# Block 1 of a two-block transformer: the arithmetic of the finished rows' layer norm on GpSimd, the context rows' mask on VectorE

## The chip, the cores and the metric

The kernel runs on one core of a Trainium2 chip. The metric is device time in microseconds (us). A core has engines that run side by side, each taking its instructions in a fixed order: PE (TensorE, matrix products and transposes; PEld is its weight load), DVE (VectorE), ACT (ScalarE), POOL (GpSimd) and SP (SyncE), which issues the transfers (DMAs) between memory and the core. Semaphores make an instruction wait for those of another engine.

## The reference

Two blocks, one after the other, on x of shape (16, 256, 512) with a context of the same shape, 16 heads of 32. Block 0 is cross attention with a mask and an MLP of width 2048. Block 1, the one that is changed, is:

```python
mask0 = 1.0 - jnp.all(x == 0, axis=2, keepdims=True).astype(x.dtype)
z = _mha(x, x, Wq1, Wk1, Wv1, mask0, causal=True)
x1 = _layernorm(x + z, ln1_g, ln1_b)
mask1 = 1.0 - jnp.all(x1 == 0, axis=2, keepdims=True).astype(x1.dtype)
z = _mha(x1, context, Wq2, Wk2, Wv2, mask1, causal=False)
x2 = _layernorm(x1 + z, ln2_g, ln2_b)
z = jnp.maximum(x2 @ fc1_w.T + fc1_b, 0.0) * mask0
z = (z @ fc2_w.T + fc2_b) * mask0
return _layernorm(x2 + z, ln3_g, ln3_b)
```

The layer norm of a row is (x - mean) / sqrt(var + eps) * gain + offset. In `_mha` the queries, keys and values are multiplied by a 0/1 mask per row; for the second attention the keys and values come from the context, so the context's rows carry mask1.

## The kernel before

**Tiles.** Two sequences of 256 rows form a group: 512 rows, four row tiles of 128 rows by 512 columns (t = 0 to 3). There are NG = 8 groups. Block 0 runs first, its attention up to about 700 us and its MLP up to about 1390. Then block 1's attention: 16 jobs (`Mha`), first eight of self-attention, one a group, then eight of cross-attention. Then block 1's MLP.

**Two streams woven together.** A job has eight units (two sequences by four sets of four heads). The main stream (`Attention.stream`) goes head by head through all jobs: scores on PE (L414), their minimum (with the causal mask, L429, or plain, L425) on DVE, the exponential on ACT (L439), transposes on PE (L455), copies to `pt` by ACT (L461) or, for one head of four in cross jobs, by DVE (L459), and at the end of a unit the product with the values (L474). The score banks in PSUM are two, so PE can be two heads ahead of the minimum and the exponential. Beside it, `feed(n)` does the projections of a job ahead of its attention: the transposes of its input rows (L283), the projections (L264), the count of valid keys (`lengths`, L1404 to L1412, DVE). `weave` interleaves the two by costs in the program text.

**The order.** PE's instructions run in the order in which the program names them (`manual_schedule` for PE alone). The other engines' orders, SP's included, are written by the tile scheduler, which places an instruction by its own estimate of the times at which its inputs are ready. On the chip every engine then keeps that order.

**The end of a unit.** `Mha.scale` (L1450, L1451) makes the reciprocal of the row sums times the mask, `finish` (L1463 to L1472) transposes the unit's result, multiplies it into `zz` on DVE (L1465) and adds it to x on GpSimd (L1472; `zz` has two buffers). After four units, half a job, two row tiles are complete, and two calls of `norm` are put into the list `later`, of which the main stream takes one per head.

**The norm of the finished rows.** `norm(t)` calls `layer_norm`: `ln_stats` (L244, L245, L247 on DVE, then the power -0.5 on GpSimd, L248), then two instructions on DVE over 128x512, L257 ((x - mean) * gain) and L258 (x * rstd + offset). In self jobs `nonzero` (L1368, DVE) reads the finished row into a scratch tile `junk` and leaves the row's mask in m1. Then SP stores the row (L1441). The store is read back eight jobs later by the cross job of the group, or by the MLP. The x tile itself is one of three, used again three jobs later.

**The context rows.** `context_rows` fetches a 128x512 row tile `cx` (L1551; three buffers, shared with `junk`), `context` multiplies it by the row mask on GpSimd (L1558) and transposes it on PE (L283). In a cross job the fetches for the next job go out as soon as a buffer is free, right after the transposes of this job's rows.

**Weights.** At the change from self to cross, and from cross to the MLP, weights are fetched into `wst` (a tag with six buffers that `pt` shares) and split into two parts on GpSimd (L195, L198).

Of the kernel before, what the change touches and what calls it, by code (L numbers as in the profile page):

```python
# [16 lines left out]
ALU = mybir.AluOpType  # L17
# [14 lines left out]
NG = B // NB  # L32
# [10 lines left out]
def kernel(ctx: ExitStack, tc: tile.TileContext, a, out):  # L43
# [7 lines left out]
    nc = tc.nc  # L51
# [22 lines left out]
    for t, at in ((0, 0), (1, P)):  # L74
        w = (t + 1) * P
        nc.gpsimd.affine_select(
            out=tri[:, at : at + w],
# [10 lines left out]
    for i in range(NB):  # L88
        own = hmask[:, i, i * HPC : (i + 1) * HPC]
        nc.gpsimd.memset(own, 1.0)  # L90
        for base, step in ((0, 1), (D - 1, -1)):
            nc.gpsimd.affine_select(
                out=own,
# [146 lines left out]
    def ln_stats(pool, src, n=4):  # L240

        st = pool.tile([P, nc.vector.BN_STATS_DIM], F32, tag="bnst", name="st")
        mv = pool.tile([P, nc.vector.BN_AGGR_DIM], F32, tag="bnmv", name="mv", bufs=n)
        nc.vector.bn_stats(st, src)  # L244
        nc.vector.bn_aggr(mv, st)  # L245
        rstd = pool.tile([P, 2], F32, tag="bnrs", name="rstd", bufs=n)
        nc.vector.tensor_scalar(rstd[:, 0:1], mv[:, 1:2], EPS, None, ALU.add)  # L247
        nc.gpsimd.tensor_tensor(out=rstd[:, 1:2], in0=rstd[:, 0:1], in1=nhalf, op=ALU.pow)  # L248
        return mv[:, 0:1], rstd[:, 1:2]

    def normalize(pool, dst, src, n=4):
        mean, rstd = ln_stats(pool, src, n)
        nc.vector.tensor_scalar(dst, src, mean, rstd, ALU.subtract, ALU.mult)

    def layer_norm(pool, x, gain, offset):
        mean, rstd = ln_stats(pool, x)
        nc.vector.scalar_tensor_tensor(x, x, mean, gain, ALU.subtract, ALU.mult)  # L257
        nc.vector.scalar_tensor_tensor(x, x, rstd, offset, ALU.mult, ALU.add)  # L258
# [9 lines left out]
    def sbuf(ph, name, bufs, side=None):  # L268
        return ph.enter_context(
            tc.tile_pool(name=name, bufs=bufs, side=side, reuse_waits="tile")  # L270
        )
# [7 lines left out]
    def transposed(dst, src, t, tag="mm"):  # L279

        ps = bank(tag, "ps_t").rearrange("p (c n) -> p c n", n=P)
        for c in range(KC):
            nc.tensor.transpose(ps[:, c, :], src[:, ts(c, P)], ident)  # L283
        split(ps, (dst[0][:, :, ts(t, P)], dst[1][:, :, ts(t, P)]))
        return 4 * T_PASS
# [274 lines left out]
    def phase1():  # L560
# [122 lines left out]
        def normal(g, tag, t):  # L683
            x = fetched.pop((g, tag, t), None)
            if x is None:
                x = fetch(g, tag, t)
            normalize(pool, x, x)
            return x
# [184 lines left out]
    class Mlp0:  # L873
# [111 lines left out]
        def normal(self, x):  # L985
            normalize(self.small[0], x, x, self.small[1])
# [379 lines left out]
    def nonzero(junk, src, m):  # L1366

        nc.vector.tensor_scalar(  # L1368
            junk, src, 0.0, None, ALU.not_equal, ALU.max, accum_out=m
        )  # L1370
# [49 lines left out]
    def block1(mlp0):  # L1420
        tables, more = {}, {}

        class Mha(Job):
# [10 lines left out]

            def norm(self, t):
                x, table = self.x[:, t, :], tables["ln2" if self.cross else "ln1"]
                layer_norm(pool, x, table[:, 0, :], table[:, 1, :])
                if not self.cross:
                    junk = pool.tile([P, C], F32, tag="t512", name="junk", bufs=3)
                    nonzero(junk, x, m1[:, self.g, t : t + 1])  # L1440
                nc.sync.dma_start(  # L1441
                    out=xd[3 if self.cross else 2][self.g][ts(t, P), :], in_=x
                )
# [40 lines left out]
        def inputs(tag):  # L1484
            return pair(mlp0.ins, tag)
# [36 lines left out]
        pool = sbuf(ctx, "work3", 2)  # L1522
# [25 lines left out]
        def context_rows(n, t):  # L1548
            if n < len(jobs) and jobs[n].cross and (n, t) not in cxs and t < G:
                cx = cxs[n, t] = pool.tile([P, C], F32, tag="t512", name="cx", bufs=3)  # L1550
                nc.sync.dma_start(out=cx, in_=of("ctx", jobs[n].g)[:, t, :])  # L1551

        def context(n, t):
            job = jobs[n]
            if t == 0:
                job.c_t = inputs("c_t")
            cx = cxs[n, t]
            nc.gpsimd.tensor_scalar(cx, cx, job.m[:, t : t + 1], None, ALU.mult)  # L1558
            cost = transposed(job.c_t, cx, t)
            context_rows(n, t + 3)  # L1560
            return cost
# [20 lines left out]
        def feed(n):  # L1582
# [5 lines left out]
            for c in range(KC):  # L1588
                ps = yield from project_t(w["q"].w, c, job.x_t)
                q, hl = halves(pool, 0, 2)  # L1590
                q0s[c] = first_token(pool, tok0, ps)
                split(ps, hl, scale=-SC if job.cross else None)
                att.keep(job, c, 0, q)
                if job.cross:
                    for t in FRONTS[c]:
                        context_rows(n, t)
                        yield context(n, t)
# [146 lines left out]
```

## Time and profile before

| | before |
|---|---|
| median of 3 runs (lowest, highest) | 2738.64 us (2737.24, 2739.17) |
| the profiled execution | 2737.66 us, span 2735.9 us |
| granted TensorE clock, mean | 0.992 |
| DVE, norm of the finished rows L257, L258 | 0.742 us each (median) |
| GpSimd, mask of a context row L1558 | 1.572 us (median), 32 times |
| GpSimd, addition of 128x512 L1656 | 1.300 us (median) |
| GpSimd, residual addition of 128x256 L1472 | 0.735 us (median) |
| GpSimd, power L248 | 0.657 us (median) |

A row of a group of instructions names the line, engine, operation and tiles and gives the duration of one. In a timeline, a line begins with the start and the duration in us, and in brackets stands how long the engine had been idle and what released it. In a list of waits, the three numbers are the total in us, the times, and the longest. L257 and L258 are in the helper that block 1's MLP also calls (32 of their 96 rows), so they are told apart by their time. Idle time of an engine costs something only if the chain of work that sets the end runs through it.

### The profile page before, as it was taken

How to read it: one execution, taken by the hardware profiler on the slowest of the kernel's cores; microseconds unless marked ns; L12 is line 12 of the kernel's file. 1: busy time of each engine (PE TensorE's matmuls, PEld its weight loads, DVE VectorE, ACT ScalarE, POOL GpSimd, SP SyncE). 2: the span in 40 equal slices, each digit the busy share in tenths (PEclk: the TensorE clock that was granted, in tenths of full speed). 3: DMA queues.
4: the chain of work that ended last, by engine and by line, in shares of the span. 5: the costliest groups of instructions: out<-in, count | busy, mean ns of one | idle time of the engine just before them, and what ended most of it. 6: DMA issues, size and time to landing. Idle time of an engine off the chain costs nothing.

```text
span 2735.9 us, 56705 instructions
## 1 busy us (share of the span) xinstructions
PE 2655.3 (97%) x19030; PEld 2244.6 (82%) x19030; DVE 2051.8 (75%) x5963; ACT 1817.4 (66%) x5278; POOL 604.7 (22%) x676
## 2 busy tenths in 40 slices
PE   8999999999899999999989999999999999999998
PEld 6777777777799999999977887877777777777787
DVE  8776667757846569999957777777678777777887
ACT  4877777778555555444547788887777777777522
POOL 2222212114401100111211111115222222114334
PEclk9999999999999999999999999999999999999999
DMA  6666556556323344443474656667566665565221
GB/s 231 189 193 182 170 170 192 183 169 174 112 114 134 126 165 167 164 169 135 160 232 163 198 191 192 196 195 224 179 198 193 190 192 184 183 187 163 100 93 51
DMA packets 287808, 465.40 MB, mean 170 GB/s; under 512 B 36256, under 2 KB 188320, under 8 KB 279328
## 3 DMA queue, kind: packets, MB, share of 16 engines
q1 hardware_dynamic: 287520, 461.78, 52.5%
q8 instruction: 153, 2.51, 0.4%
q14 instruction: 135, 1.11, 0.1%
HBM read 284.97 MB, written 176.69 MB: 169 GB/s over the span
## 4 chain that ended last, share of the span: by engine, by line
PE 78%; DVE 12%; DMA 4%; issue 3%; ACT 2%; POOL 1%; SPq 0%; POOLq 0%; DVEq 0%; ACTq 0%
PE ps_p L264 18%; PE ps_v L264 15%; PE down L1142 10%; PE ps_pt L455 9%; PE ps_s L414 6%; PE ps_z L474 6%; PE up_sc L1026 5%; PE up_pt L1026 3%; PE up_mm L1026 3%; PE ps_t L283 2%; DVE e L429 1%; DVE st L244 1%; DVE x L258 1%; DVE c_t L145 1%; PE ps_z L1463 1%
## 5 line engine op out<-in xcount | busy, mean ns | idle before, releaser
L439 ACT ACTIVATE e<-e,mn 128x256 f32<-128x256 f32 (+1 forms) x1024 | 487.6, 481 | 64.9 <-DVE mn L429 62.5
L461 ACT COPY pt<-ps_pt 128x512 f32<-128x512 f32 (+1 forms) x696 | 378.4, 547 | 171.6 <-PE ps_pt L455 160.3
L455 PE MATMUL ps_pt<-ident,e 128*128 128x128 f32 x2816 | 435.5, 273 | 14.1 <-DVE lbias L1405 8.1
L455 PEld LDWEIGHTS ps_pt<-ident,e 128*128 128x128 f32 x2816 | 336.0, 140 | 53.6 <-DVE lbias L1405 6.2
L414 PE MATMUL ps_s<-stack 97*128 97x256 f32 (+1 forms) x1536 | 331.7, 297 | 12.6 <-ACT e L439 5.3
L414 PEld LDWEIGHTS ps_s<-stack 97*128 97x128 f32 (+1 forms) x1536 | 268.8, 190 | 72.7 <-ACT e L439 12.3
L439 ACT ACTIVATE e<-ps_s,mn 128x256 f32<-128x256 f32 x512 | 241.3, 484 | 52.4 <-DVE mn L425 44.2
L1142 PE MATMUL down<-w_h,c_t 128*128 128x256 f32 x900 | 256.1, 285 | 5.4 <-DVE c_t L145 5.4
L1472 POOL TENSOR_TENSOR x<-x,zz 128x256 f32<-128x256 f32 x128 | 95.8, 749 | 727.7 <-DVE zz L1465 663.9
L1142 PE MATMUL down<-w_h,x_t 128*128 128x256 f32 x868 | 246.6, 284 | 1.4 <-ACT x_t L144 1.4
L1142 PE MATMUL down<-w_l,x_t 128*128 128x256 f32 x868 | 246.9, 284 | 0.0
L429 DVE CUSTOM_DVE_ANT_0 e<-mb,ps_s 128x256 f32<-128x256 bf16 x512 | 192.5, 414 | 71.3 <-PE ps_s L414 70.3
L248 POOL TENSOR_TENSOR rstd<-rstd,nhalf 128x1 f32<-128x1 f32 x192 | 142.4, 747 | 380.0 <-DVE rstd L247 379.7
L264 PE MATMUL ps_p<-x_t,q_h 128*128 128x512 f32 x640 | 216.2, 419 | 4.2 <-DVE qk L131 2.1
L425 DVE TENSOR_REDUCE mn<-ps_s 128x2 f32<-128x512 f32 x256 | 175.2, 684 | 49.2 <-PE ps_s L414 47.0
L474 PE MATMUL ps_z<-pt,v 128*32 128x256 f32 (+1 forms) x3072 | 200.3, 370 | 7.2 <-DVE pt L459 4.3
L429 DVE CUSTOM_DVE_ANT_0 e<-tri,ps_s 128x128 f32<-128x128 f32 (+1 forms) x512 | 160.1, 346 | 55.7 <-PE ps_s L414 53.7
L439 ACT ACTIVATION_READ_ACCUMULATOR e<-e,mn 128x1 f32 x1024 | 197.6, 193 | 0.0
L1142 PEld LDWEIGHTS down<-w_h,c_t 128*128 128x128 f32 x900 | 171.9, 191 | 7.2 <-DVE c_t L145 7.2
L474 PEld LDWEIGHTS ps_z<-pt,v 128*32 128x32 f32 x3072 | 82.8, 109 | 104.8 <-issue 27.5
L1142 PEld LDWEIGHTS down<-w_h,x_t 128*128 128x128 f32 x868 | 167.2, 193 | 1.8 <-ACT x_t L144 1.6
L1142 PEld LDWEIGHTS down<-w_l,x_t 128*128 128x128 f32 x868 | 166.0, 191 | 0.0
(256 smaller groups left out, 7218.6 us busy)
## 6 DMA issues: line engine op xcount, KB each, us to landing
stack<-d SPq DMA_DIRECT2D x1152, 128.0 KB
d<-qk SPq DMA_DIRECT2D x192, 512.0 KB
hid<-ho SPq DMA_DIRECT2D x32, 1024.0 KB
raw<-hid SPq DMA_DIRECT2D x32, 1024.0 KB
x<-xd SPq DMA_DIRECT2D x128, 256.0 KB
xd<-x SPq DMA_DIRECT2D x96, 256.0 KB
xin<-in_x_dram SPq DMA_DIRECT2D x32, 256.0 KB
xr<-in_x_dram SPq DMA_DIRECT2D x32, 256.0 KB
```

The lines of the kernel that those rows point to most:

```text
L248: nc.gpsimd.tensor_tensor(out=rstd[:, 1:2], in0=rstd[:, 0:1], in1=nhalf, op=ALU.pow)
L264: nc.tensor.matmul(ps, w[p], x[q], start=(k == 0 and i == 0), stop=(k == kc - 1 and i == 2))
L414: nc.tensor.matmul(ps[:, t, :], u.st[: self.rows, 0, j, ts(t, P)], u.st[: self.rows, 1, j, :], start=True, stop=True,)
L425: nc.vector.tensor_reduce(mn, ps, AX.X, ALU.min)
L429: nc.vector.tensor_tensor_reduce(out=e[:, at], in0=bias[t], in1=ps[:, t, : job.width[t]], scale=-SC, scalar=BIG, op0=ALU.add, op1=ALU.min, ...
L439: nc.scalar.activation(e[:, at], ps[:, t, :] if bias is None else e[:, at], AF.Exp, bias=mn[:, t : t + 1], scale=-1.0, accum_out=u.rs[:, t ...
L455: nc.tensor.transpose(pp[:, ts(x, P)], e[:, at : at + P], ident)
L461: nc.scalar.copy(pt[:, :n], pp[:, :n])
L474: nc.tensor.matmul(z[ts(j, D), w[0] * P :], job.v[u.i * NT + mc][:, u.c * P + j * D : u.c * P + (j + 1) * D], u.pt[j][:, x0 * P : (x0 + le ...
L1026: nc.tensor.matmul(ps[:, mm, :], w[p][:, k, :], x[q][:, k, :], start=(first and mm == k == j == 0), stop=(k == 1 and j == 2), skip_group_c ...
L1142: nc.tensor.matmul(ps[:, t, :], x[p][:, mm, ts(t, P)], w[r][:, bo, :], start=(q == mm == t == j == 0), stop=(q == self.NS - 1 and mm == 1 ...
L1472: nc.gpsimd.tensor_tensor(out=xv, in0=xv, in1=zz, op=ALU.add)
```

## The change

The norm of the finished rows in block 1's attention keeps its statistics where they are. The arithmetic on the row becomes three instructions on GpSimd, (x - mean) * rstd, times gain, plus offset, for all jobs but the last (the cross job of group 7), which keeps the two instructions on DVE. The MLP's norm is not touched. The mask of the context rows moves from GpSimd to DVE.

```diff
+    def layer_norm_pool(pool, x, gain, offset):
+
+        mean, rstd = ln_stats(pool, x)
+        nc.gpsimd.tensor_scalar(x, x, mean, rstd, ALU.subtract, ALU.mult)
+        nc.gpsimd.tensor_tensor(out=x, in0=x, in1=gain, op=ALU.mult)
+        nc.gpsimd.tensor_tensor(out=x, in0=x, in1=offset, op=ALU.add)
...
             def norm(self, t):
                 x, table = self.x[:, t, :], tables["ln2" if self.cross else "ln1"]
-                layer_norm(pool, x, table[:, 0, :], table[:, 1, :])
+                last = self.cross and self.g == NG - 1
+                norm = layer_norm if last else layer_norm_pool
+                norm(pool, x, table[:, 0, :], table[:, 1, :])
...
             cx = cxs[n, t]
-            nc.gpsimd.tensor_scalar(cx, cx, job.m[:, t : t + 1], None, ALU.mult)
+            nc.vector.tensor_scalar(cx, cx, job.m[:, t : t + 1], None, ALU.mult)
             cost = transposed(job.c_t, cx, t)
```

## The prediction

> **What bounds the kernel now.** I read the page's engine shares first, then busy time by stage, then each wait of PE in block 1's attention (about 1395 to 2560 us), then what VectorE and GpSimd did just before those waits.
>
> The page's first part, and the busy times of two self-attention jobs and three cross-attention jobs (window, its length, then each engine's busy us, granted clock, DMA share, GB/s):
>
> ```profile
> PE 2655.3 (97%) x19030; PEld 2244.6 (82%) x19030; DVE 2051.8 (75%) x5963; ACT 1817.4 (66%) x5278; POOL 604.7 (22%) x676
> ...
> 1539.44:1605.73 66.29, 65.42 (x480) 52.91 (x481) 50.65 (x237) 53.23 (x185) 9.60 (x12) 1.00 0.60 192
> 1605.73:1672.02 66.29, 65.41 (x481) 52.91 (x481) 50.64 (x237) 53.25 (x185) 9.56 (x12) 1.00 0.61 192
> 2106.18:2180.77 74.59, 73.20 (x528) 58.01 (x528) 58.18 (x145) 55.63 (x180) 15.09 (x17) 1.00 0.60 185
> 2180.77:2255.62 74.85, 73.25 (x529) 58.01 (x529) 58.48 (x145) 55.63 (x180) 15.21 (x17) 1.00 0.59 184
> 2255.62:2330.32 74.70, 73.27 (x529) 58.05 (x529) 58.23 (x145) 55.74 (x180) 15.38 (x17) 1.00 0.59 185
> ```
>
> PE is busy for 65.4 of 66.3 us in a self job and 73.2 of 74.7 in a cross job, at a granted clock of 1.00. No edit of VectorE or GpSimd work can win more than those 0.9 and 1.4 us a job. The reader should see this ceiling first: GpSimd has room (10 to 15 us busy a job), but VectorE's total is not the bound either. Only the moments when PE stands still count.
>
> PE's timeline in those jobs (idle before the instruction and its releaser in brackets):
>
> ```profile
> 1605.73 0.47 PE L414 MATMUL ps_s<-stack 97*128 97x256 f32 x2 [0.61 <-DVE rr L1451]
> 1607.27 0.50 PE L414 MATMUL ps_s<-stack 97*128 97x256 f32 x2 [0.27 <-DVE mn L429]
> ...
> 2180.77 0.66 PE L455 MATMUL ps_pt<-ident,e 128*128 128x128 f32 x4 [0.86 <-DVE lbias L1405]
> 2214.57 0.51 PE L414 MATMUL ps_s<-stack 97*128 97x256 f32 x2 [0.29 <-ACT e L439]
> ```
>
> These waits come back every job at the same place: just after the norms of a job's second half (both kinds), and of its first half (cross only). VectorE and GpSimd before the 2214.57 wait:
>
> ```profile
> 2211.08 1.57 POOL L1558 TENSOR_SCALAR cx<-cx,m 128x512 f32<-128x512 f32 x1 [5.50 <-DMA cx<-in_ctx_dram]
> 2212.62 1.08 POOL L248 TENSOR_TENSOR rstd<-rstd,nhalf 128x1 f32<-128x1 f32 x2
> 2213.22 1.41 DVE L258 SCALAR_TENSOR_TENSOR x<-x,rstd,ln 128x512 f32<-128x512 f32 x2 [0.53 <-POOL rstd L248]
> ```
>
> GpSimd stood at the context row's transfer, the two rstd powers stood behind the mask, VectorE's L258 behind the powers, and the score minimum L425 behind L258. Before 2180.77 VectorE is busy almost without a break from 2167.8 on, with two L257 and two L258 in the run (2.9 us of it).
>
> **The change, part by part.** The sum is against the profiled execution, 2737.66 us (span 2735.9), 1.0 below the median 2738.64.
>
> *Second-half waits, removed.* 60 of the 64 attention rows lose L257 and L258 on VectorE: 60 x 2 x 0.742 = 89 us busy, 2.97 us per pair of rows (a half job). The waits behind them: self, five jobs x (0.60+0.27) + 0.74 = 5.1 us; cross, five x 0.87 + 1.16 + 1.32 (the first cross job) + 0.64 = 7.5 us. A pair's 2.97 us is more than any of these, so I take all 5.1, and 6.1 of the 7.5, since the 1.32 (a copy L459 late at 2031, five us after L258) may be another backlog.
>
> *First-half waits in cross jobs, exchanged.* They sum to 6 x 0.30 + 0.18 + 0.74 + 0.47 = 3.2 us. The power no longer stands behind the mask and L258 is gone, but the mask on VectorE now stands at the same transfer. On GpSimd that idle was 63.8 us over 25 of 32 rows. On VectorE it would be only what other work leaves: nearest row, block 0's bn_stats on freshly fetched rows, which does exactly this.
>
> ```profile
> DVE st L244 <- DMA xin<-in_ctx_dram: 6.2, 8, 1.4
> DVE st L244 <- DMA xin<-in_x_dram: 4.9, 4, 1.5
> ...
> PE ps_s L414 <- DVE mn L429: 0.2, 1, 0.2
> ```
>
> Between 100 and 400 us VectorE lost 11.1 us this way, yet PE waited 0.2 us in all. The mask itself: 32 x 0.543 (L253, the same form with two scalars) = 17 us on VectorE, 32 x 1.57 = 50 off GpSimd. Bounds for PE: a gain of 3.2 (all first-half waits go) to a loss of 12 (see the second rival). I take 0.
>
> *The norm on GpSimd.* Per row one tensor_scalar with two scalar columns: no such row exists; bounds 1.57 (one operation, L1558) and 3.1 (twice that); I take 1.6, nearest in form. Two tensor_tensor of 128x512: 1.30 each (L1656, L198). So 4.2 us a row, 252 in all, 8.4 per pair behind two powers (1.8). GpSimd goes from 9.6 to about 26 us in a 66.3 us self job and from 15.2 - 6.3 + 16.8 to about 26 in a 74.7 us cross job: not a bound. Queued behind it on GpSimd: the residual additions L1472, one every 8.3 us; one of them starts up to 8 us late, and zz has two buffers, so VectorE's next zz does not wait. The store L1441 follows at the pair's end, 5 us later than L258 ends now; SP is in order and stack loads stand behind it, but stack has three tiles, two units (some 16 us) ahead. The next readers of x, the slot of three jobs later and the rows read back eight jobs later, have most of a job. Cost 0 on these covers; gone, the SP delay of 5 us at 30 half jobs would be paid.
>
> *A new wait in the self jobs.* nonzero L1368 reads the finished row, so VectorE, in its fixed order, waits for GpSimd if the order puts it too early. Order other than PE's is not program order (two rows' statistics stand side by side in the trace), so it is placed by an estimate of when the row is ready. Nearest rows: L258 after the power on GpSimd, 5.1 us idle over 96 rows, 0.05 a row. Bounds: 0, and one row's chain (4.2 us) per pair, in 16 pairs. I take 32 x 0.05 = 1.7, because the waits of VectorE for GpSimd that this trace has are all small.
>
> *The hand-over between self and cross (1865 to 1940).* PE waits 2.31 us at 1917 for a mask that stood behind the value weight's split on GpSimd. On VectorE it is 1.0 us shorter and off that queue; but the norms of the same moment (powers at 1904.5) now add 8.4 us there, and the raw weight rows hold buffers that the transposed scores also use. Between +2.3 and -4.2; I take 0. The split of the last two weights (2456 to 2492) has the same exposure and no PE wait now; 0.
>
> *Contention.* L257 takes 1.85 us instead of 0.74 five times in the last stage, each time beside a GpSimd addition, and the cast of tok 0.61 instead of 0.17 beside a mask at 2218.6. Most VectorE work in attention reads PSUM, and L425 shows 0.68 beside the masks as elsewhere. 0; bound 64 casts x 0.44 = 28 us of VectorE, in gaps.
>
> Sum: 5.1 + 6.1 - 1.7 = 9.5; 2737.7 - 9.5 = 2728.2, and 1.0 for the median: 2729.
>
> [...]
>
> **The rivals.**
> 1. *VectorE waits for GpSimd (slower).* If L1368 is ordered d us before the row is ready, each of 16 self pairs loses about d - 2.97 (the pair's saving), on top of today's waits. With the 6.1 won in cross jobs, it ends above no change from d = 2.97 + 6.1/16 = 3.4 us and clearly slower (5.5 us) from 3.7. At d = 4.2 it costs 16 x 1.23 = 20: 2738.6 + 20 - 6 = 2753. For it: the masks stand ahead of ready powers in GpSimd's order, so estimates of readiness are early by over 1 us for transfers. Against: none of the trace's waits for GpSimd arithmetic shows that.
> 2. *The masks eat the gain (same).* Three context rows arrive in the first-half norms. Idle of 1.0 each there and four masks (2.2) make 5.2 against 2.97 + 0.53 freed: 1.7 us x 7 jobs = 12, against 9.5 won: 2741. For: the 3.2 us from issue to landing (2207.7 to 2211.1). Against: block 0.
> 3. *What is late next (same).* PE's waits at L414 are released by ACT's exp; ACT has 55.6 of 74.7. If half of each wait stays, 4.7 us are won: 2734.
>
> **How the numbers follow.** Forecast 0.47, its own range 2718 to 2733 (low end: 5.1 + 7.5 + 3.2 + 2.3 = 18.1 won, 2720, less 2). Rivals 2 and 3 together 0.23, rival 1 and its kin on SP 0.30. What a measurement of this kernel can tell from no change is about 0.2%, 5.5 us: faster is below 2733.2, slower above 2744.1. The range runs from 2717 to 2753, the price of rival 1.
>
> **What would show it.** Right: no L257/L258 before 2560 but for the last job; the waits at L1451/L429 after self norms and at L1405 after cross norms gone; self jobs near 65.5 and cross jobs near 73.8 us; VectorE near 45 and 54.5 a job. Wrong: VectorE idle before L1368 released by GpSimd's x, or before the mask released by cx's transfer, each over 1 us, with PE idle behind it; SP waiting long at L1441 with stack loads late.

## The result and the profile after

The changed kernel takes 2757.92 us (median of 4 runs, 2756.14 to 2767.42); the kernel before took 2738.9 us beside it (4 runs, 2737.24 to 2739.55). The ratio is 1.0077, with a 95% interval of 1.0064 to 1.0089: slower by 0.8%. The forecast of 2729 us had the wrong sign, and the time lies above the range (2717 to 2753). The profiled execution took 2758.18 us, with a span of 2756.5 and a mean granted clock of 0.986; its span is 20.6 us longer than the one before.

The page's engine shares, the windows of two self jobs, and four windows at the hand-over from the self jobs to the cross jobs. Columns as before: window, length, busy us of PE, PEld, DVE, ACT and POOL with the instructions of each, granted clock, DMA share, GB/s.

```profile
PE 2658.9 (96%) x19030; PEld 2251.3 (82%) x19030; DVE 2031.3 (74%) x5875; ACT 1812.0 (66%) x5278; POOL 810.7 (29%) x824
...
1540.33:1605.95 65.62, 65.18 (x481) 52.86 (x481) 50.35 (x229) 52.63 (x185) 26.46 (x25) 1.00 0.62 194
1605.95:1671.57 65.62, 65.16 (x481) 52.86 (x481) 50.37 (x229) 52.62 (x185) 26.50 (x25) 1.00 0.63 194
1865.00:1940.00 75.00, 54.60 (x362) 42.72 (x363) 42.21 (x184) 40.92 (x141) 39.22 (x38) 0.84 0.54 169
1910.90:1926.10 15.20, 0.00 (x0) 0.00 (x0) 3.56 (x13) 1.91 (x7) 11.16 (x10) 0.60 0.47 152
1926.10:1935.00 8.90, 8.84 (x54) 6.87 (x55) 3.21 (x18) 3.90 (x13) 0.33 (x1) 0.73 0.27 95
1935.00:1945.00 10.00, 10.00 (x76) 7.90 (x78) 6.33 (x34) 8.56 (x32) 1.16 (x2) 1.00 0.59 191
```

The periodic part did what the forecast said: a self job went from 66.29 to 65.62 us, with GpSimd busy for 26.5 us, the figure foreseen. The largest loss is in a place that has no period: for 15.2 us at the hand-over PE ran nothing at all. The same 75 us window (1865 to 1940) held 66.79 us of PE work before; now it holds 54.60.

PE's timeline of the changed kernel (start, duration, what ran, and in brackets the idle time before it with its releaser), its longest standstills and a self job's new small wait:

```profile
1605.95 0.55 PE L462 MATMUL ps_pt<-ident,e 128*128 128x128 f32 x3 [0.44 <-ACT pt L468]
...
1883.60 1.49 PE L481 MATMUL ps_z<-pt,v 128*32 128x256 f32 x10 [3.63 <-ACT pt L468]
...
1926.16 1.12 PE L290 MATMUL ps_t<-ident,cx 128*128 128x128 f32 x4 [15.36 <-DVE cx L1567]
1927.21 1.51 PE L481 MATMUL ps_z<-pt,v 128*32 128x256 f32 x16
...
2008.73 1.11 PE L290 MATMUL ps_t<-ident,cx 128*128 128x128 f32 x4 [6.72 <-DVE cx L1567]
...
2504.62 1.11 PE L462 MATMUL ps_pt<-ident,e 128*128 128x128 f32 x4 [2.92 <-ACT pt L468]
...
2541.59 0.91 PE L290 MATMUL ps_t<-ident,x 128*128 128x128 f32 x4 [2.20 <-DMA x<-xd]
```

The lines of the new kernel's code stand 7 to 9 further down than before: L462 was L455, L468 was L461, L1567 is the mask, L1375 the non-zero test (L1368), L1450 the store of a finished row (L1441), L1560 the fetch of a context row (L1551). The three new instructions of the norm are L258, L259 and L260. The two long waits are for a masked context row, behind the norms that end the last two self jobs (counted from 0: jobs 6 and 7). The mask is only the last link. What came before it, on GpSimd, on VectorE and in SP's queue:

```profile
1908.74 0.61 POOL L195 CAST v_h<-wst 128x512 fp32r<-128x512 f32 x1 [2.51 <-DMA wst<-in_w_v_dram]
1909.34 4.15 POOL L258 TENSOR_SCALAR x<-x,mv,rstd 128x512 f32<-128x512 f32 x2
1913.45 0.72 POOL L1481 TENSOR_TENSOR x<-x,zz 128x256 f32<-128x256 f32 x1
...
1915.91 2.49 POOL L259 TENSOR_TENSOR x<-x,ln 128x512 f32<-128x512 f32 x2
1918.36 1.27 POOL L198 TENSOR_TENSOR v_l<-wst,v_h 128x512 fp32r<-128x512 f32 x1
1919.58 2.48 POOL L260 TENSOR_TENSOR x<-x,ln 128x512 f32<-128x512 f32 x2
```

```profile
1920.88 0.69 DVE L1375 TENSOR_SCALAR_CACHE_REDUCE junk<-x 128x512 f32<-128x512 f32 x1 [8.11 <-POOL x L260]
...
1925.62 0.49 DVE L1567 TENSOR_SCALAR cx<-cx,m 128x512 f32<-128x512 f32 x1 [2.83 <-DMA cx<-in_ctx_dram]
```

```profile
1920.87 1.56 SPq L1450 DMA_DIRECT2D xd<-x  x2
1922.84 0.33 SPq L1560 DMA_DIRECT2D cx<-in_ctx_dram  x1
```

In the kernel before, SP issued the same two with the fetch 10.6 us earlier:

```profile
1910.31 0.98 SPq L1441 DMA_DIRECT2D xd<-x  x2
1912.24 0.33 SPq L1551 DMA_DIRECT2D cx<-in_ctx_dram  x1
```

Read from the end: PE waits for the mask, the mask for the row's transfer, the transfer was issued at 1922.84. The list of SP's waits names the non-zero test's tile `junk` for that fetch (L1560, 0.3 us) and GpSimd's L260 for the stores ahead of it (L1450, 7.2 us, the longest 6.4): SP, which keeps its order, stood at the stores. In the code, `junk` and the context rows `cx` are tiles of one tag, `t512`, with three buffers between them. So the fetch of a context row waits until a test has run, the test until GpSimd has finished the norm, and the norm runs among the casts and subtractions that split the value weight (L195, L198). Before the second wait the two tests ran at 2003.70 and 2004.39, and the fetches left from 2004.60 on (in the kernel before: a test at 1987.12, fetches from 1988.05 on). No wait of the fetch for a test is listed there, so for the second wait the chain is read from the order alone; e3 below tests it.

### The profile page after: what moved, and what is told of

Read it like the earlier page. It is cut to its first block, busy times and chain, and to the rows that moved or that the text cites. A ratio compares the mean times of both kernels' runs of the same rounds, so it can differ in the third digit from the quotient of the medians.

```text
span 2756.5 us, 56610 instructions
## 1 busy us (share of the span) xinstructions
PE 2658.9 (96%) x19030; PEld 2251.3 (82%) x19030; DVE 2031.3 (74%) x5875; ACT 1812.0 (66%) x5278; POOL 810.7 (29%) x824
## 5 line engine op out<-in xcount | busy, mean ns | idle before, releaser
L468 ACT COPY pt<-ps_pt 128x512 f32<-128x512 f32 (+1 forms) x696 | 377.6, 546 | 152.2 <-PE ps_pt L462 132.9
L462 PE MATMUL ps_pt<-ident,e 128*128 128x128 f32 x2816 | 436.3, 273 | 14.0 <-ACT pt L468 11.7
L462 PEld LDWEIGHTS ps_pt<-ident,e 128*128 128x128 f32 x2816 | 336.7, 141 | 54.2 <-ACT pt L468 16.8
L248 POOL TENSOR_TENSOR rstd<-rstd,nhalf 128x1 f32<-128x1 f32 x192 | 126.2, 663 | 398.7 <-DVE rstd L247 352.7
```

The source lines that it names most:

```text
L462: nc.tensor.transpose(pp[:, ts(x, P)], e[:, at : at + P], ident)
L468: nc.scalar.copy(pt[:, :n], pp[:, :n])
```

## The experiments

All edits are against the changed kernel, and each ratio is to runs of the kernel before on the same chip. For the experiments the medians of the kernel before are 2743.57 to 2744.55 us, some 5 us above the 2738.9 of the result, so an expectation in us, which was written against 2738.9, is best read by its ratio. To compare places, each profiled execution is cut at three instructions that all kernels share: M1, PE's short wait near 1470 in the first self job; M2, PE's first projection behind the second context row's transposes in the second cross job (2060.16 in the kernel before); M3, the same five cross jobs later (2433.33). So "M1 to M2" holds the rest of the self jobs, the hand-over and the first cross job; "M2 to M3" holds five cross jobs (9 to 13), and the last column the last two cross jobs (14 and 15) with the splitting of the MLP's weights, and the MLP.

| kernel | ratio (95%) | to M1 | M1 to M2 | M2 to M3 | M3 to end |
|---|---|---|---|---|---|
| before | 1 | 1470.4 | 589.7 | 373.2 | 302.6 |
| after | 1.0077 (1.0064, 1.0089) | 1468.3 | 607.7 | 369.4 | 311.0 |
| e1 norm alone | 1.0056 (1.0043, 1.0068) | 1477.0 | 606.6 | 364.0 | 311.1 |
| e2 mask alone | 1.0057 (1.0040, 1.0073) | 1468.9 | 590.4 | 390.3 | 303.7 |
| e3 junk's own buffer | 0.9995 (0.9986, 1.0004) | 1471.2 | 584.2 | 372.9 | 309.1 |
| e4 jobs 6, 7 on VectorE | 1.0033 (1.0020, 1.0045) | 1470.5 | 590.5 | 372.6 | 313.8 |
| e5 norm alone, own buffer | 0.9998 (0.9989, 1.0006) | 1471.1 | 591.6 | 365.4 | 313.7 |
| e6 norm of cross jobs alone | 0.9975 (0.9966, 0.9985) | 1470.8 | 589.0 | 364.8 | 312.3 |
| e7 as e5, less job 14 | 0.9971 (0.9960, 0.9983) | 1471.7 | 590.5 | 365.9 | 308.0 |
| e8 mask alone, placed | 1.0018 (1.0009, 1.0026) | 1470.5 | 588.4 | 382.3 | 303.7 |
| e9 own buffer, mask placed | 0.9965 (0.9952, 0.9978) | 1469.0 | 583.4 | 366.0 | 309.9 |
| e10 as e6, less job 14 | 0.9963 (0.9949, 0.9977) | 1470.2 | 588.9 | 364.7 | 304.4 |
| e11 e9, less job 14 | 0.9935 (0.9923, 0.9948) | 1471.8 | 586.9 | 366.0 | 302.9 |

"To M1" is work that the edits touch only in its last 5 us, where the first norm begins, and it spreads from 1468.3 to 1477.0; M1 to M2 in e9 and e11, whose texts differ only in a later job, differs by 3.5. So a cell of the other three columns says nothing below some 3.5 us, and the first column less still; the ratios, which go over several executions, do. Each row of cells is one execution: that of e9 is the shortest of its 7 (2730.01 us, median 2734.93), that of e11 the longest of its 6 (2729.42, median 2725.42), so rows are compared by place and not by sum. The loss of the change by place: 18.0 at the hand-over, 8.4 after M3, less 3.8 gained in the cross jobs and 2.1 of that spread before M1.

**e1, the norm alone.** The mask goes back to GpSimd.

```diff
-            nc.vector.tensor_scalar(cx, cx, job.m[:, t : t + 1], None, ALU.mult)
+            nc.gpsimd.tensor_scalar(cx, cx, job.m[:, t : t + 1], None, ALU.mult)
```

> The norm's arithmetic on GpSimd as in the change, the context rows' mask back on GpSimd. Theory A (the late context row: at the hand-over from self to cross jobs the fetch of a context row needs a buffer, or a place in SP's queue, behind a norm that GpSimd finishes late): the two waits of PE for the context rows (15.4 and 6.7 us in the changed kernel) stay, the mask adds 1 us each: 2756 to 2764. Theory B (VectorE stands 8 us at the row's non-zero test for GpSimd, and everything of PE's behind it): same, 2755 to 2760. Theory C (the mask on VectorE is what holds the rows up): both waits go, 2728 to 2736.

Measured: 2757.93 us. PE's long waits are there just the same, released by a mask that now runs on GpSimd:

```profile
1933.58 1.12 PE L290 MATMUL ps_t<-ident,cx 128*128 128x128 f32 x4 [16.51 <-POOL cx L1567]
2018.17 1.12 PE L290 MATMUL ps_t<-ident,cx 128*128 128x128 f32 x4 [8.34 <-POOL cx L1567]
```

So the mask's engine does not hold the rows at the hand-over. In the five cross jobs, on the other hand, the norm alone wins 9.2 us (373.2 to 364.0): 1.8 a job, where the forecast counted 0.87. PE stands idle for 1.3 us from 2070 to 2430 (360 less 358.72 busy), against 6.7 before (360 less 353.31): the waits of both halves are gone, 0.9 and 0.3 us a job. That is 5.4 of the gain; the rest shows only as shorter busy times of PE's instructions, whose ends are modelled, and was not traced further. PE counted 137.1 ns an instruction there (2617 of them) and 138.8 before (2545), and the five jobs take 364.0 us, where PE alone counted as busy for 365.97 before: that busy time was no floor.

**e2, the mask alone.** All rows keep VectorE's norm.

```diff
-                last = self.cross and self.g == NG - 1
+                last = True
```

> The mask on VectorE as in the change, all norms on VectorE as before. A and B: no norm is late, so no wait of more than 2.5 us at the hand-over; the mask is 1 us shorter there, and in the first half of each cross job the wait of the powers behind the mask goes and a wait of VectorE for the transfer comes: 2734 to 2742. C: the waits of 15 and 7 us stay: above 2750.

Measured: 2755.5 us. Only C allowed such a time, but C's two waits are not there. The hand-over is whole (590.4), and the cross jobs take 17.1 us more, 3.5 a job. VectorE's waits from 2060 to 2440, where the kernel before has none for `cx`, and PE's in the same window (total us, times, longest):

```profile
DVE cx L1567 <- DMA cx<-in_ctx_dram: 16.9, 15, 3.3
```

```profile
PE ps_s L421 <- ACT e L446: 6.1, 5, 1.8
PE ps_pt L462 <- DVE lbias L1412: 4.3, 5, 0.9
PE ps_z L481 <- DVE pt L466: 3.7, 3, 1.5
PE ps_s L421 <- DVE tok L1384: 3.5, 2, 1.9
```

PE's waits in this window sum to 18.4 us, and to 7.6 in the kernel before. VectorE stands at the rows' transfers, and what is queued behind it in its fixed order reaches PE late: the copies, the exponent's inputs, the token copies. The mask is no side matter of the change: taken alone it costs 0.57% of the time.

**e3, a buffer of its own for `junk`.** The test's output is thrown away, so it may have another type and one buffer; `cx` and the rest keep the three.

```diff
-                    junk = pool.tile([P, C], F32, tag="t512", name="junk", bufs=3)
+                    junk = pool.tile([P, C], BF16, tag="junk", name="junk", bufs=1)
```

> The change, with one difference: the scratch tile that the non-zero test writes has one buffer of its own in bf16 instead of sharing three with the context rows (nothing reads it, so the output is the same). A, by the shared buffers: the context rows are fetched well before they are needed, both waits of PE go (22 us, and some 2 of slow clock behind them): 2730 to 2738. A, by SP's queue: the fetches stay behind the stores of the rows: above 2750. B: VectorE still waits 8 us at the test for GpSimd, so the larger wait stays in good part: 2744 to 2758.

Measured: 2740.93 us, 0.9995. Both long waits are gone, with the norm still on GpSimd in the same jobs. The window of the hand-over, and SP's fetches in it:

```profile
1865.00:1940.00 75.00, 68.27 (x471) 53.61 (x470) 55.02 (x230) 53.76 (x188) 44.16 (x43) 0.98 0.71 211
```

```profile
1911.58 0.35 SPq L186 DMA_DIRECT2D wst<-in_w_v_dram  x1
1912.03 0.42 SPq L1560 DMA_DIRECT2D cx<-in_ctx_dram  x1
...
1919.32 1.89 SPq L1560 DMA_DIRECT2D cx<-in_ctx_dram  x2
...
1931.02 0.38 SPq L1450 DMA_DIRECT2D xd<-x  x1
```

A fetch leaves at 1912.0, as in the kernel before, and the stores of the finished rows come after the fetches, not ahead of them. GpSimd's norm is later than in the changed kernel (its last L260 ends at 1927.4, there at 1922.1), and no engine is listed as waiting for it between 1895 and 1945. That shows the cause of the largest loss: the shared buffers, and not GpSimd's speed by itself. The other type does not shorten the test itself (0.68 us in both). What the run does not separate are the links behind the buffers. With the buffer the orders changed too: SP's stores went behind the fetches, and VectorE's test of these rows went to 1930.91, after the norm. How much of the 15.4 us was the fetch's wait for the test, how much SP's stand at the stores and how much VectorE's 8.1 us at the test is open; all three went together. The run also suggests what the norm is worth in the self jobs and the first cross job once it holds nothing up: 589.7 to 584.2.

**e4, the norms of jobs 6 and 7 on VectorE**, the last two self jobs, whose rows stand at the hand-over.

```diff
-                last = self.cross and self.g == NG - 1
+                last = self.g >= NG - (1 if self.cross else 2)
```

> The change, but the norms of the last two self jobs stay on VectorE (all other jobs' as in the change). If the whole loss is at the hand-over (A or B): 2730 to 2738, with the gain of the jobs around it (0.6 us for each self job, about 1 for each cross job). If it is spread over the jobs: above 2750.

Measured: 2752.26 us. The hand-over is cured (590.5), the total is not: the last column holds 11.2 us more than before (313.8), and the 372.6 of the cross jobs is no gain on 373.2, where the norm alone reached 364.0. The expectation left out the second hand-over and the mask's price.

**e5, e1's and e3's edits together**, to see the norm without the mask and without the shared buffer.

> Norm on GpSimd in all jobs but the last, the mask on GpSimd as before, the test's scratch tile with a buffer of its own (bf16, nothing reads it). If the loss is a sum of three places (the shared buffers at the first hand-over, about +22 us; the mask on VectorE in cross jobs, about +5; the weights' split behind the norm at the second hand-over, +8), only the third is left here: self jobs and hand-over 5 us shorter than before, cross jobs 9, the end 8 longer: ratio to before 0.996 to 0.999. If the places are not independent (the cross jobs' gain without the mask only came because the hand-over had run late): 1.000 or above.

Measured: 0.9998, and a gain was expected. The cross jobs gain 7.8 us, near e1's 9.2, but the hand-over takes 7.4 us more than in e3 (591.6 to 584.2). The trace has waits there of 2.4 us at a score for a token copy and 3.5 at a row read back (`x<-xd`), each once. They explain little of the 7.4, as all of PE's waits from 1465 to 2065 sum to 18.6 us in e5 and to 17.0 in e3. More of it is the clock: in the stretches 1865 to 1900, 1900 to 1940 and 1940 to 2000 the granted clock is 0.90, 0.96 and 0.97 in e5, and 0.95, 1.00 and 1.00 in e3, by these figures an estimated 35 x 0.05 + 40 x 0.04 + 60 x 0.03 = 5 us. Why PE stands at other places with the mask on GpSimd is not settled.

**e6, the norm on GpSimd in cross jobs alone, the mask on GpSimd.**

```diff
-                last = self.cross and self.g == NG - 1
+                last = not self.cross or self.g == NG - 1
```

(and e1's edit)

> Norm on GpSimd in the cross jobs but the last, self jobs' norms on VectorE, the mask on GpSimd, buffers as in the change. By the sum of places: nothing at the first hand-over (no test waits for GpSimd), cross jobs 9 us shorter, the second hand-over 8 longer: 0.999 to 1.001. If the sharing of buffers were not what makes the rows late, 15 us and more would stay: 1.005.

Measured: 2737.63 us, 0.9975. The cross jobs' gain stands alone (364.8), and 312.3 in the last column shows where the rest goes: that stretch takes 309 to 314 us in all seven kernels that have job 14's norm (the last cross job but one) on GpSimd.

**e7, e5 with job 14 back on VectorE** (`last = self.cross and self.g >= NG - 2`, with e1's and e3's edits).

> As the run with norm on GpSimd, mask on GpSimd and own scratch buffer, but the last two cross jobs' norms stay on VectorE, so that no norm stands beside the split of the last weights on GpSimd. By the sum of places all three losses are away: 5 + 8 or more won: ratio 0.993 to 0.997, faster than before and than the change. If the second hand-over's loss is not the split behind the norm: as the run without this exemption.

Measured: 2737.22 us, 0.9971. M3 to end takes 308.0, less than e5's 313.7, though not the 303 to 304 of e8, e10 and e11.

**e8, the mask alone, placed.** As e2, but each mask is ordered behind the last subtraction of a split (`latest["l"]`), where the row's transfer has had time to land.

```diff
+            with tc.issue_after(latest["l"].ins):
+                nc.vector.tensor_scalar(cx, cx, job.m[:, t : t + 1], None, ALU.mult)
```

> The mask alone on VectorE (all norms on VectorE), but each mask may not be issued before the split of the transpose ahead of it, so that it runs just before its own transposes, some 10 us and more after the row has landed for most rows. If the loss of the mask alone is VectorE standing at transfers in its fixed order: it goes, ratio 0.999 to 1.002. If it is VectorE's own time for the masks (0.49 us each): 1.004 to 1.007 as before.

Measured: 2746.76 us, 1.0018. VectorE's 16.9 us at the transfers are gone to the last one, and the cross jobs take 382.3 in place of 390.3: 8.0 of the 17.1 us. The other 9.1 remain, in waits like these:

```profile
2134.88 0.66 PE L290 MATMUL ps_t<-ident,cx 128*128 128x128 f32 x4 [1.18 <-DVE rstd L247]
2141.95 0.51 PE L421 MATMUL ps_s<-stack 97*128 97x256 f32 x2 [1.60 <-ACT e L446]
```

So about half of the mask's price was the wait for transfers. The rest is in waits behind VectorE's statistics and behind the exponent, in a stretch in which the norm's four instructions and the mask stand together on VectorE. That the two crowd each other is supported by e9 below, where the norm leaves VectorE and the placed mask costs nothing that the table can show (366.0 to e5's 365.4).

**e9, e3's and e8's edits on the change as it is**: both parts kept, the shared buffers and the wait for transfers taken away.

> The change with two differences: the test's scratch tile has its own buffer, and each mask is issued behind the split of the transpose ahead of it. If what VectorE loses at the masks is the wait for the transfers, the cross jobs come near the 72.8 us of the norm alone instead of 74.6 and the whole is 5 to 8 us below the run with the own buffer alone: 0.996 to 0.998. If it is the masks' place in a crowded stretch of VectorE whatever the transfers: no change, 0.999 to 1.001.

Measured: 2734.93 us, 0.9965. The whole change now gains. What is left is after M3:

```profile
2475.24 0.66 PE L462 MATMUL ps_pt<-ident,e 128*128 128x128 f32 x4 [2.92 <-ACT pt L468]
...
2513.38 0.83 PE L290 MATMUL ps_t<-ident,x 128*128 128x128 f32 x4 [2.73 <-DMA x<-xd]
```

**e10, e6 with job 14 back on VectorE** (`last = not self.cross or self.g >= NG - 2`, with e1's edit).

> Norm on GpSimd in the first six cross jobs alone, all other norms on VectorE, the mask on GpSimd, buffers as in the change. By the sum of places, the cross jobs' 8 us are won and neither hand-over is touched: ratio 0.994 to 0.997, and the stretch from the last of the six cross marks to the end near the 302.6 us of before instead of 311 to 314. If the end is longer for another reason than the norm beside the last weights' split: 0.9975 as the run with all cross jobs but one.

Measured: 2733.31 us, 0.9963. M3 to end takes 304.4 in place of e6's 312.3, and both waits of the last fence are gone. From 2425 to 2560 PE's waits sum to 4.7 us, in e6 to 8.8, which leaves 3.8 of the 7.9 us. They are found in the clock: it was 0.91 from 2480 to 2500 and 0.94 from 2500 to 2530 in e6, behind its two long waits, and 1.00 in both stretches in e10, an estimated 20 x 0.09 + 30 x 0.06 = 3.6 us. That job 14's norm on GpSimd costs this is shown: e5 against e7 gives 5.7 us and e9 against e11 7.0 in the same column, and their ratios fall by 0.0027 and 0.0030. From e6 to e10 the ratio falls by 0.0012 alone, with intervals that overlap; e10's cells are from the shortest of its 5 executions. By which link is not: its norm stands beside the splits of the MLP's first weights, and the copies L468 write tiles that share buffers with the raw weights. At the first hand-over the trace names that link (L468 waits 3.3 us for `k_l` and 3.7 for `v_l`, both L198 on GpSimd), at this one it does not.

**e11, e9 with job 14 back on VectorE**: everything learned in one kernel.

```diff
-                last = self.cross and self.g == NG - 1
+                last = self.cross and self.g >= NG - 2
```

(and e3's and e8's edits)

> The change with own scratch buffer, placed masks, and the last two cross jobs' norms (not the last one's alone) on VectorE. If the three places add up: the stretches of the run with the first two differences stay (583 and 366 us) and the end falls from 310 to 303 to 305: span 2721 to 2724, ratio 0.992 to 0.996. If the end stays near 310, the loss at the second hand-over is not the norm beside the weights' split: 0.9965 again.

Measured: 2725.42 us (6 runs, 2723.94 to 2729.42) against 2743.83 there: 0.9935 (0.9923 to 0.9948). It is faster than the kernel before by 0.65% and than the changed kernel by about 1.4% (0.9935 / 1.0077). Each of the last three columns is within 4 us of its lowest.

## Why the prediction was wrong

*The failed step* is "The hand-over between self and cross (1865 to 1940) ... Between +2.3 and -4.2; I take 0." It measured 18.0 us lost over M1 to M2, net of what the self jobs won, with single waits of 15.4 and 6.7 us, the second of them at 2008.73, past the stretch that the step looked at. The step looked for the danger in the right moment and among the right instructions: it saw the norms join the value weight's split, and buffers shared with the transposed scores (that part came true: 3.6 us at 1883.60, behind a copy that waited 3.3 us for the key weight's split; the kernel before stood 3.1 us near there, at 1884.43, for `lbias`). But it priced GpSimd's delay by GpSimd's own work, 8.4 us, as a thing that only the norm's readers would feel. It never asked which tile the reader of the row writes. The non-zero test writes `junk`, `junk` shares three buffers with `cx`, and a delayed test is a delayed fetch. The SP delay, which the prediction named ("rival 1 and its kin on SP") and put at 5 us for every half job if its covers were gone, showed at this one place: SP stood 6.4 us at the store, with the fetch behind it. In the kernel before this chain was 10 us early and the trace named it only once, as a 0.9 us wait of SP for `junk`; in the middle of the self jobs it does not exist, as the first context row is fetched at 1874.6.

*First-half waits, "I take 0"*, failed second. The mask alone cost 3.5 us a cross job (e2), beyond the lower bound: 17.1 over five jobs against a bound of 12 over seven. Rival 2 had the mechanism, at 1.7 a job, and half of it is shown as such (e8). The row that decided against it, block 0's statistics on freshly fetched rows, comes from a stage in which PE follows VectorE less closely; that this is why it misled is argued, not shown. Within the whole change the norm's removal pays for most of it: the cross jobs went from 373.2 to 369.4, where the norm alone reached 364.0.

*"The split of the last two weights has the same exposure and no PE wait now; 0"* measured 8.4 us in the changed kernel; e6 against e10 puts 7.9 on job 14's norm, waits and slower clock together.

*The second-half waits* were right in kind. They went: in a self job the 0.87 us gave way to a single new wait of 0.44 us behind ACT's copy, and the job is 0.67 us shorter, the other 0.24 in PE's busy time (65.42 to 65.18); in a cross job of e1 all of them went. The prediction has the halves the wrong way round: its waits at 1605.73 and 2180.77 follow the norms of a job's first half, those at 2214.57 the second's (block 1's first norm, at 1465, comes behind its fourth residual addition). No term of the sum hangs on the name.

*The ceiling*, "No edit of VectorE or GpSimd work can win more than those 0.9 and 1.4 us a job", was reached or passed in the cross jobs of seven kernels: 1.8 us a job in e1, 1.4 to 1.7 in e5, e6, e7, e9, e10 and e11. PE's instructions were counted as shorter there, as e1 shows.

*The norm's size on GpSimd* was low by a tenth: 2.09 + 1.30 + 1.30 = 4.7 us a row, not 4.2, as the first step with two scalar columns took 2.09 and not 1.6. The load it makes, 26 us a self job, was foreseen and is no bound. "Cost 0 on these covers" held in the periodic jobs and nowhere else.

*Contention, "0"*, and with it the sign "VectorE near 45 and 54.5 a job", was wrong by more than its bound of 28 us. A self job lost four L257 and four L258 (5.9 us) on VectorE, and yet VectorE was busy for 50.35 us after 50.65; over the whole program its busy time fell by 20.5 us, where 60 x 2 x 0.742 less 32 masks of 0.49 make 73. Small instructions of VectorE took longer beside GpSimd's norm, this one 1.10 us:

```profile
1608.03 1.10 DVE L1460 TENSOR_TENSOR rr<-rr,m 128x8 f32<-128x8 f32 x1
```

```profile
1606.58 2.53 POOL L259 TENSOR_TENSOR x<-x,ln 128x512 f32<-128x512 f32 x2
```

In four self jobs of the kernel before (1539 to 1805) this multiplication of 128x8 never took more than 0.17 us. Here it began beside the second L259 and ended with it. What this cost PE no run separates: the changed self job is shorter all the same.

*Rival 1*, VectorE waiting for GpSimd at the test in 16 self pairs, did not occur: from 1395 to 1850 there is no wait of VectorE for GpSimd's norm. The 1.7 us taken for it was not needed. The rival's sign was right by another mechanism: a single wait at the hand-over, and with a buffer of its own for the test (e3) it is gone.

*Rival 3* holds in part: a self job's 0.44 us is such a next link.

## What to carry to other kernels

Before an operation moves to a slower engine (here 4.7 us a row on GpSimd for 1.5 on VectorE), follow not only who reads its result but which buffers its readers hold, and what transfer waits for those buffers; a throw-away tile in a shared tag is a hidden link. Price the change at every place where the schedule changes its kind (the first and last job of a loop, weights being loaded beside it), since the periodic part can be right to a few tenths of a microsecond and the total wrong by twenty. An operation on a freshly fetched tile did best here on the engine that PE follows less closely, or far enough behind the fetch: on VectorE, with the norm there too, the mask cost 17.1 us over five cross jobs, and 9.1 when it was placed (e2, e8). And count the instructions that run beside the moved ones: in a self job VectorE's busy time fell by 0.3 us, where the norm's two instructions had taken 5.9.

## What was not expected of the hardware

PE ran nothing from 1910.9 to 1926.1. The granted clock was 1.00 in the first 2.9 us of this, 0.50 in the rest and in the first 4.7 us of work behind it, and only then 0.99:

```profile
1913.80:1926.10 12.30, 0.00 (x0) 0.00 (x0) 1.87 (x5) 0.48 (x1) 8.26 (x8) 0.50 0.42 142
1926.10:1930.80 4.70, 4.64 (x25) 3.10 (x26) 0.70 (x2) 0.96 (x2) 0.00 (x0) 0.50 0.51 179
1930.80:1935.00 4.20, 4.20 (x30) 3.78 (x30) 2.52 (x16) 2.95 (x11) 0.33 (x1) 0.99 0.00 0
```

16 matmuls `ps_z` took 1.51 us at 1927.21 and 0.86 us at 1936.97. By 4.7 x 0.5, about 2.4 us of the loss at the hand-over is an estimate of what the slower clock cost on top of the wait. So this stand was paid twice: by its own 15.2 us, and by the 4.7 us of work at a clock of 0.50 behind it. Shorter stands were followed by a slower clock too: in e6 those of 2.92 us (to 2484.52) and 1.92 us (to 2521.62), with 0.91 and 0.94 in the stretches given under e10. The first 16 matmuls `ps_z` behind them took 2.10 us (at 2485.11) and 1.52 us (at 2525.41); in e10, without such a stand, 16 took 1.07 us (at 2481.80).

GpSimd and VectorE did not run independently in the self jobs: beside the norm on GpSimd, small VectorE instructions on tiles in SBUF took up to 1.1 us in place of 0.17 (L1460, 128x8), and up to 1.45 in place of at most 0.46 (L1419, before L1412, 8x256).

GpSimd's tensor_scalar of 128x512 took 2.09 us with two operations and two scalar columns, 1.57 with one operation (the mask before), and a plain cast of the same size 0.61. The second operation and its column together were not free; which of the two costs the 0.5 us no run separates.
